# A fifth batch of early keys and values, and a shorter last routing, in a two-layer decoder kernel on one core

## The chip, the core and the metric

The kernel runs on one core of a Trainium2 chip. A core has five engines that each work through their own queue in order: TensorE (PE in the profile; its weight loads are shown as PEld) multiplies matrices and transposes, VectorE (DVE), ScalarE (ACT) and GpSimd (POOL) work on elements, and SyncE (SP) mostly issues DMAs. They wait for each other by semaphores. The metric is the device time of one execution in microseconds (us), taken as the median of several runs. Everything here is computed in 32-bit floating point; the profile shows each such matmul as two records, so "x8" in a matmul row is four matmuls.

## The reference

The input `x` has 16 batches of 112 tokens with 256 features, the context `ctx` 16 batches of 375 rows. Two pre-norm layers follow each other; the change lies in the second layer, and around the place where the two meet. Cut to what matters:

```python
x = x + L0_attn(layernorm(x))               # linear attention
x = x + L0_xattn(layernorm(x), ctx)         # 16 heads
x = x + L0_ffn(layernorm(x))                # 16 experts, top 2, plus a shared one
x = x + L1_attn(layernorm(x))               # 16 heads of 64
x = x + L1_xattn(layernorm(x), ctx, g1, b1, g2, b2, Wq, Wkv, Wout, bout)   # 8 heads of 64
x = x + L1_ffn(layernorm(x))                # 8 experts, top 2, capacity 33

def L1_xattn(x, context, ...):
    xn, cn = layer_norm(x, g1, b1), layer_norm(context, g2, b2)
    q = xn @ Wq
    k, v = split(cn @ Wkv, 2)               # per batch: 375 x 512 each
    return softmax(q k^T / 8) v @ Wout + bout

def L1_ffn(x, ...):                         # per batch of 112 tokens
    top, ei = top_k(x @ router_w + router_b, 2)
    probs = softmax(top)
    pos = place of the token in its expert's list (first choices of all tokens come first)
    buf[ei, pos] = x                        # 8 experts x 33 places; later ones are dropped
    out[e] = silu((buf[e] @ w_c_fc + b) * (buf[e] @ w_gate + b)) @ w_c_proj + b
    return sum over the two choices of probs * out[ei, pos]
```

## The kernel before

The residual `x` stays in on-chip memory, with 112 tokens on the partitions. The stages run one after another over the 16 batches.

**Layer 0's experts and the join.** Tokens are gathered into blocks of 128 rows of one expert each; 36 blocks (`NB_MEAN`) are worked through by `blocks(0)` in a hand-written order for PE and DVE (`fetch`, `turn`, `up`, `turn_act`, `down`): SP loads a block (`xb`), PE multiplies, ACT scales the result (`os`), and POOL scatters its rows to DRAM (`yo`, by `scatter`, line 1063). Behind it stands `If n_used > NB_MEAN`, which on these inputs isn't taken; each engine loads the count and branches. Then the pools of this stage are closed, and layer 1 opens its own in the same memory. Layer 1 begins with `combine(b)` (line 1530): SP loads the two rows of each token back (`yb`), DVE adds them to `x`, and the norm of layer 1 follows (`norm_one`: line 234 and 235 on DVE, 242 and 243 on POOL, 238 on DVE, the transposes of line 267 on PE).

**Keys and values ahead.** The keys and values of layer 1's cross-attention depend on `ctx` alone. For the batches in `AHEAD` (0, 4, 8, 12) they are computed during layer 0, with `c_ahead` (three transposes and one ACT operation per half), `k_ahead` (four pieces of two matmuls, copied by ACT, line 401) and `v_ahead` (three pieces of two matmuls, line 414), and ACT stores them to DRAM (`kd`, `vd`; lines 403 and 416). `norm_ahead` norms the context rows.

**Layer 1's cross-attention.** It has 32 units, two per batch (`n` counts them, `u` is 0 or 1), each for four heads. In the loop at line 1600 and on, a unit emits: `turned` (transposes of the probabilities, line 1493), `scores` of the next unit (line 1461; then the row maximum on DVE, line 1472, exp on ACT, line 1473, the reciprocal on DVE, line 1482, and the division of the 112x375 probabilities on POOL, line 1484, four per unit), one entry popped from the list `after`, the projection of the batch before (`project`), the query pieces, the pieces that make the next batch's keys and values if it isn't in `AHEAD` (`c_piece`, `k_piece`, `v_piece`: six transposes of the context, 8 key and 6 value matmuls per batch over two units), and `values` (line 1509). If the next batch is in `AHEAD`, SP loads its keys and values instead (`k_load`, `v_load`).

**Routing.** The list `after` holds the routing work: `routed(b)` (router logits of batch b; after every fourth batch also `route1`, the top two of eight), `places` (the place of each token in its expert, from two prefix-sum matmuls and, per rank k, a chain of small DVE operations), and `dispatch1(b)` for four batches, which builds a 112x264 matrix of ones (`dm`, from `slot_rows`) and multiplies it by the normed tokens (`xn`), so that the tokens land at their places (`first_in` for the first 12 places of every expert, `more_at` for the other 21). `places` also sums, per expert, how many tokens stand beyond the first 12 (`more`, `need`); `ranks` orders the experts by that count, and SP needs its result to load the weights of the four busiest experts. The last routing comes after the units: what is left in `after`, `routed(15)`, `places`, `slot_rows`, `ranks` and `dispatch1` of batches 12 to 15, and then the first expert (`hidden`, from line 1826 on). `jobs` is a list of small tasks, one popped per step of the expert loop. The order on PE and DVE in these parts is that of the code.

## Time and profile before

| | us |
|---|---|
| median of three runs (1603.69 to 1607.48) | 1604.29 |
| time of the profiled execution | 1611.35 |
| its span | 1609.6 |
| PE busy | 1501.8 (93%) |
| DVE busy | 964.1 (60%) |
| ACT busy | 577.9 |
| POOL busy | 483.1 (30%) |
| last matmul of layer 0's blocks ends | 608.4 |
| first matmul of layer 1 | 621.0 |
| last projection of the cross-attention ends | 1316.7 |
| first matmul of the first expert | 1342.7 |

The span is the time from the first to the last instruction of one profiled execution, and the times in the rows below are counted from its start. The clock granted to PE was 0.973 of full speed on average. In a timeline row stand: start, duration, engine, line of the code, operation, what it writes and reads, its shape, how many instructions are taken together, and in brackets how long the engine had been idle and what ended that. A row of a queue (SPq, ACTq) is the issue of a DMA, not its transfer.

### The profile page before, as it was taken

The numbers are of one execution on the slowest core, as the hardware profiler recorded it, in microseconds if no ns is written. First come the engines' busy times: TensorE is split into PE (matmuls) and PEld (weight loads), VectorE is DVE, ScalarE is ACT, GpSimd is POOL, SyncE is SP. The second block draws the span as 40 slices with busy tenths as digits, with TensorE's granted clock in tenths as the row PEclk, the third lists the DMA queues.
The fourth block names the chain that finished last, engine by engine and source line by source line (L and its number), as shares of the span: only waits on it lengthen the run. The fifth ranks groups of instructions, "written<-read, shape, count | busy, mean of one in ns | idle before, by whom it ended". The sixth has DMA issues, their size and how long they took to land.

```text
span 1609.6 us, 30346 instructions
## 1 busy us (share of the span) xinstructions
PE 1501.8 (93%) x11438; PEld 1127.5 (70%) x11438; DVE 964.1 (60%) x2649; ACT 577.9 (36%) x1437; POOL 483.1 (30%) x647
## 2 busy tenths in 40 slices
PE   7898999999988896899999989999999978999998
PEld 5776777777754585778888756666666657788786
DVE  6986777777762353976677655566575566342124
ACT  3441444444442252223333233343434323333332
POOL 5642122222115352323333344544445420000000
PEclk9999999999999897999999999999999988999999
DMA  6500322222224476200000010101010012344421
GB/s 170 143 10 21 94 67 65 67 65 65 64 76 158 130 231 214 54 24 1 1 1 2 20 56 10 49 20 48 19 30 30 1 53 79 137 178 157 147 89 48
DMA packets 84929, 116.52 MB, mean 72 GB/s; under 512 B 13433, under 2 KB 70946, under 8 KB 84778
## 3 DMA queue, kind: packets, MB, share of 16 engines
q1 hardware_dynamic: 78690, 98.25, 20.1%
q0 software_dynamic: 3312, 8.54, 1.6%
q10 hardware_dynamic: 2776, 7.72, 1.4%
q8 instruction: 95, 1.56, 0.4%
q14 instruction: 56, 0.46, 0.1%
HBM read 84.41 MB, written 22.08 MB: 66 GB/s over the span
## 4 chain that ended last, share of the span: by engine, by line
PE 76%; DVE 13%; POOL 4%; DMA 3%; issue 2%; another core or an unknown queue 1%; ACT 1%; SPq 0%; POOLq 0%; DVEq 0%; ACTq 0%
PE pT L120 49%; PE pT L785 3%; PE pT L1461 3%; PE pT L1493 2%; POOL pr L1484 2%; DVE mx L769 2%; PE pT L1509 2%; PE pT L803 2%; PE pT L767 2%; PE pT L1358 2%; PE pT L1393 2%; PE pT L1379 2%; PE pT L620 1%; DVE st L234 1%
## 5 line engine op out<-in xcount | busy, mean ns | idle before, releaser
L1484 POOL TENSOR_SCALAR pr<-pr,den 112x375 f32<-112x375 f32 x128 | 157.0, 1244 | 176.9 <-DVE den L1482 157.7
L120 PE MATMUL pT<-xnT,w_all 128*128 128x224 f32 (+2 forms) x800 | 165.3, 358 | 0.6 <-DVE xnT L269 0.5
L120 PEld LDWEIGHTS pT<-xnT,w_all 128*128 128x128 f32 x800 | 145.9, 197 | 10.2 <-issue 5.7
L794 ACT ACTIVATE pr<-pT 125x336 f32<-125x336 f32 x256 | 94.6, 456 | 126.3 <-PE pT L785 126.3
L769 DVE TENSOR_REDUCE mx<-pT 112x1 f32<-112x375 f32 x256 | 122.2, 539 | 11.3 <-PE pT L767 9.9
L1371 POOL TENSOR_TENSOR pr<-pr,den 112x448 f32<-112x448 f32 x64 | 59.9, 956 | 198.8 <-DVE den L1369 147.9
L120 PE MATMUL pT<-w_all 128*128 (+3 forms) x376 | 113.1, 453 | 1.7 <-ACT w_all L392 0.8
L120 PE MATMUL pT<-w_all,cT 128*125 128x256 f32 (+1 forms) x336 | 111.4, 475 | 0.0
L120 PE MATMUL pT<-cT,w_all 128*128 128x375 f32 x320 | 110.2, 486 | 0.0
L120 PE MATMUL pT<-w_all,xnT 128*112 128x256 f32 (+1 forms) x320 | 105.7, 477 | 1.9 <-ACT xnT L566 0.9
L120 PE MATMUL pT<-w_all,oT 128*112 128x256 f32 x448 | 106.4, 383 | 0.6 <-DVE oT L1400 0.6
L242 POOL TENSOR_SCALAR nr<-nmv 112x1 f32<-112x1 f32 x96 | 22.3, 232 | 273.7 <-DVE nmv L235 273.1
L1308 ACT COPY pT<-pT 112x448 f32<-112x448 f32 (+1 forms) x64 | 34.0, 532 | 170.9 <-PE pT L1493 88.3
L120 PEld LDWEIGHTS pT<-w_all 128*128 128x128 f32 (+2 forms) x376 | 70.2, 190 | 33.8 <-issue 4.6
L1473 ACT ACTIVATE pr<-pT,top 112x375 f32<-112x375 f32 x128 | 72.4, 572 | 56.8 <-DVE top L1472 54.4
L120 PEld LDWEIGHTS pT<-cT,w_all 128*128 128x128 f32 x320 | 59.3, 190 | 41.1 <-issue 5.8
L120 PEld LDWEIGHTS pT<-w_all,oT 128*112 128x112 f32 x448 | 75.7, 177 | 16.3 <-DVE oT L1400 1.0
L120 PE MATMUL pT<-first_in,w_all 128*128 128x192 f32 x512 | 86.6, 329 | 0.0
L120 PEld LDWEIGHTS pT<-first_in,w_all 128*128 128x128 f32 x512 | 84.4, 192 | 1.5 <-issue 0.3
L120 PEld LDWEIGHTS pT<-w_all,cT 128*125 128x125 f32 x336 | 61.1, 187 | 33.3 <-issue 22.7
L120 PEld LDWEIGHTS pT<-w_all,xnT 128*112 128x112 f32 x320 | 57.1, 183 | 35.8 <-issue 22.4
L1767 DVE SCALAR_TENSOR_TENSOR hT<-pT,vT,gt 128x192 f32<-128x192 f32 x64 | 26.7, 417 | 90.5 <-ACT gt L1766 90.4
(306 smaller groups left out, 3019.2 us busy)
## 6 DMA issues: line engine op xcount, KB each, us to landing
w_all<-in_L_ffn_w_c_fc_dram SPq DMA_DIRECT2D x12, 1024.0 KB
w_all<-in_L_ffn_w_gate_dram SPq DMA_DIRECT2D x12, 1024.0 KB
w_all<-in_L_ffn_w_c_proj_dram SPq DMA_DIRECT2D x12, 1024.0 KB
cx<-in_ctx_dram SPq DMA_DIRECT2D x32, 375.0 KB
kz<-kn SPq DMA_DIRECT2D x128, 46.9 KB
xg<-w_all SPq DMA_DIRECT2D x1, 5547.0 KB
xb<-xg SPq DMA_DIRECT2D x36, 129.0 KB
yb<-yo SPq DMA_DIRECT2D x16, 224.0 KB
```

The source lines that it names most:

```text
L120: mm(o, l, r, start=(i == 0), stop=(i == len(terms) - 1))
L767: mm(ps[i][:L, :S], qz[b % 2][r, g, :], kz[b % 2][r, g, :], start=True, stop=True)
L769: nc.vector.tensor_reduce(mx[b % 2][:, g, i, 16:17], ps[i][:L, :S], AX.X, ALU.max, negate=True)
L785: mm(pw[i][:KC, j * L : (j + 1) * L], kz[b % 2][r, g, j * KC : (j + 1) * KC], qm[r, :], start=True, stop=True,)
L794: nc.scalar.activation(pr[:, i, :], pw[i][:KC, : NKC * L], AF.Exp)
L803: mm(po[32 * i : 32 * i + 32, :L], va[b % 2][:, j, 4 * g + i, :], pr[:, i, j * L : (j + 1) * L], start=(j == 0), stop=(j == NKC - 1),)
L1308: nc.scalar.copy(dst, src)
L1358: mm(ps[k][:L, s * L : (s + 1) * L], q, kk, start=True, stop=True)
L1371: nc.gpsimd.tensor_tensor(pr[:, k], pr[:, k], bcast(den[:, k, :], L), ALU.mult)
L1461: mm(ps[2 * s + k][:L, :S], qTs[b // 2][rows(k), m, (b % 2) * L : (b % 2 + 1) * L], kTs[b][rows(k), m, :], start=True, stop=True,)
L1473: nc.scalar.activation(pr[:, i, :], ps[i][:L, :S], AF.Exp, bias=top[:, i : i + 1], scale=1.0, accum_out=den[:, i : i + 1],)
L1484: nc.gpsimd.tensor_scalar(pr[:, n, :], pr[:, n, :], den[:, n : n + 1], None, ALU.mult)
```

## The change

It has two parts. First, batch 2 joins `AHEAD`, as its fifth entry (index 4). Its keys and values are made around the join: `Wkv` is loaded a second time into a part of `xnT` that is free then, the context rows are normed during the blocks, `c_ahead` stands in the last rounds of `blocks(0)`, two key pieces before the `If`, two key pieces and the three value pieces after it. In the cross-attention, batch 1's units load batch 2's keys and values instead of making them.

Second, `places` is split. What the dispatches need stays (with `place` counted from 1, so that a subtraction goes; `kept`, the place cut at 32, moves to POOL), and the probabilities and the counts (`more`, `sums`, `need`) go to a new entry `counts`, which comes after the dispatches in the list. From unit 28 on, two entries are popped per unit. In the last routing POOL norms the tokens of batches 12 to 14, and `counts` and `ranks` become tasks of the first expert. For batch 15 the tokens normed before are used.

```diff
@@ -68,7 +68,7 @@
         "rev16": rows(E0 - np.arange(E0)),
         "rev8": rows(E1 - np.arange(E1)),
         "io8": rows(np.arange(E1)),
-        "slots": rows(np.arange(E1 * CAP)),
+        "slots": rows(np.arange(E1 * CAP + 1)),
 
         "later": np.concatenate(
             [
@@ -356,7 +356,7 @@
 
 
 
-    AHEAD = (0, 4, 8, 12)
+    AHEAD = (0, 4, 8, 12, 2)
     kd = {b: dr.tile([128, 4, S], F32, tag=f"kd{b}", name=f"kd{b}") for b in AHEAD}
     vd = {b: dr.tile([KC, NKC, 512], F32, tag=f"vd{b}", name=f"vd{b}") for b in AHEAD}
 
@@ -381,7 +381,7 @@
         if c == 0:
             acTs[i] = (
                 kap[0].tile([128, 2, S], F32, tag="acT", name="acT", bufs=1)
-                if i % 2
+                if i % 2 or i == 4
                 else w_all[:, 2 * WR + 4864 : 2 * WR + 4864 + 2 * S].rearrange("p (c s) -> p c s", c=2)
             )
         pt = bank()
@@ -397,7 +397,7 @@
         if m == 0:
             akv[i] = kz[0] if i == 0 else kap[0].tile([128, 4, S], F32, tag="ak", name="ak")
         pk = bank()
-        mm_sum(pk[:, :S], [(wkv_a[0][:, c, m * 128 : (m + 1) * 128], acTs[i][:, c, :]) for c in range(2)])
+        mm_sum(pk[:, :S], [(wkv_a[i // 4][:, c, m * 128 : (m + 1) * 128], acTs[i][:, c, :]) for c in range(2)])
         nc.scalar.copy(akv[i][:, m, :], pk[:, :S])
         if m == 3:
             nc.scalar.dma_start(kd[AHEAD[i]], akv[i])
@@ -410,18 +410,18 @@
                 else kap[0].tile([KC, NKC, 512], F32, tag="av", name="av")
             )
         pv = bank()
-        mm_sum(pv[:KC, :], [(acTs[i][:, c, j * KC : (j + 1) * KC], wkv_a[0][:, c, 512:]) for c in range(2)])
+        mm_sum(pv[:KC, :], [(acTs[i][:, c, j * KC : (j + 1) * KC], wkv_a[i // 4][:, c, 512:]) for c in range(2)])
         nc.scalar.copy(akv[i][:, j, :], pv[:KC, :])
         if j == NKC - 1:
             nc.scalar.dma_start(vd[AHEAD[i]], akv[i])
 
     ahead = [
         f
-        for i in range(len(AHEAD))
+        for i in range(4)
         for f in (
             [lambda i=i, m=m: k_ahead(i, m) for m in range(4)]
             + [lambda i=i: v_ahead(i, 0)]
-            + [lambda i=i, c=c: c_ahead(i + 1, c) for c in range(2)] * (i + 1 < len(AHEAD))
+            + [lambda i=i, c=c: c_ahead(i + 1, c) for c in range(2)] * (i < 3)
             + [lambda i=i, j=j: v_ahead(i, j) for j in (1, 2)]
         )
     ]
@@ -1103,6 +1103,11 @@
                     if j in (12, 17, 22):
                         with tc.issue_after(got.ins):
                             w_qkv.extend(load_w(2 * WR + 2048 * i, [t["L1_attn_W_qkv"][i]]))
+                    if j == 24:
+
+                        wkv_a.append(xnT[:, :, NT - 1024 :])
+                        with tc.issue_after(got.ins):
+                            nc.sync.dma_start(wkv_a[1], rows_of(t["L1_xattn_Wkv"]))
 
             def turn(j):
                 pt = bank()
@@ -1153,16 +1158,27 @@
                         turn_act(n - 2)
                     if begin <= n - 3:
                         down(n - 3)
+                    if begin == 0 and n == stop - 6:
+                        norm_ahead(4)
+                    if begin == 0 and n in (stop, stop + 1):
+                        c_ahead(4, n - stop)
 
 
             w_qkv = []
             stop = NB_MEAN
             blocks(0)
+            for m in range(2):
+                k_ahead(4, m)
         n_used = nc.values_load(used[0:1, 0:1], min_val=0, max_val=NB0)
         with tc.If(n_used > NB_MEAN):
             with tc.manual_schedule(engines={mybir.EngineType.PE, mybir.EngineType.DVE}):
                 stop = NB0
                 blocks(NB_MEAN)
+        with tc.manual_schedule(engines={mybir.EngineType.PE}):
+            for m in range(2, 4):
+                k_ahead(4, m)
+            for j in range(NKC):
+                v_ahead(4, j)
     cstack.close()
     f0s.close()
     rp = pool(ctx, "route", 1)
@@ -1223,13 +1239,6 @@
         bs = slice(4 * q, 4 * q + 4)
         (oh0, v0), (oh1, v1) = top_two(lp, lg1[:, bs, :], E1, const("rev8", L))
 
-        p0, ex = prob[0][:, bs], prob[1][:, bs]
-        nc.vector.tensor_sub(ex, v1, v0)
-        nc.scalar.activation(ex, ex, AF.Exp)
-        nc.vector.tensor_scalar(p0, ex, 1.0, None, ALU.add)
-        nc.vector.reciprocal(p0, p0)
-        nc.vector.tensor_mul(ex, ex, p0)
-
         oh = [o.rearrange("p b n -> p (b n)") for o in (oh0, oh1)]
 
         def places():
@@ -1239,9 +1248,8 @@
             mm_sum(pc[:L, 4 * E1 : 8 * E1], [(before, oh[1]), (ones[:L, :L], oh[0])])
             b1 = lambda name: lp.tile([L, 4], F32, tag=f"rt_{name}", name=name, bufs=1)
             tmp = lp.tile([L, 4, E1], F32, tag="rt_tmp", name="tmp", bufs=1)
-            sums = lp.tile([L, E1], F32, tag="rt_sums", name="sums", bufs=1)
             for k in range(2):
-                pos, ok, more = b1(f"pos{k}"), b1(f"ok{k}"), b1(f"more{k}")
+                pos, ok = b1(f"pos{k}"), b1(f"ok{k}")
                 o3 = (oh0, oh1)[k]
                 kept, ei = pos1[k][:, bs], exp1[k][:, bs]
                 nc.vector.tensor_tensor(
@@ -1252,18 +1260,32 @@
                 nc.vector.tensor_reduce(ei, tmp, AX.X, ALU.add)
                 nc.vector.tensor_scalar(ok, pos, CAP - 0.5, None, ALU.is_lt)
 
-                nc.vector.tensor_scalar(kept, pos, float(CAP - 1), None, ALU.min)
-
-                nc.vector.scalar_tensor_tensor(pos, ei, float(CAP), kept, ALU.mult, ALU.add)
-                nc.vector.scalar_tensor_tensor(pos, pos, 1.0, ok, ALU.add, ALU.mult)
-                nc.vector.tensor_scalar(place[k][:, bs], pos, -1.0, None, ALU.add)
-
-                nc.vector.tensor_scalar(more, kept, P0 - 0.5, None, ALU.is_gt)
-                nc.vector.tensor_tensor(tmp, o3, bcast(more, E1), ALU.mult)
+                to = place[k][:, bs]
+                nc.vector.scalar_tensor_tensor(to, ei, float(CAP), pos, ALU.mult, ALU.add)
+                nc.vector.scalar_tensor_tensor(to, to, 1.0, ok, ALU.add, ALU.mult)
+
+                nc.gpsimd.tensor_scalar(kept, pos, float(CAP - 1), None, ALU.min)
+
+        def counts():
+
+            p0, ex = prob[0][:, bs], prob[1][:, bs]
+            nc.vector.tensor_sub(ex, v1, v0)
+            nc.scalar.activation(ex, ex, AF.Exp)
+            nc.vector.tensor_scalar(p0, ex, 1.0, None, ALU.add)
+            nc.vector.reciprocal(p0, p0)
+            nc.vector.tensor_mul(ex, ex, p0)
+
+            b1 = lambda name: lp.tile([L, 4], F32, tag=f"rt_{name}", name=name, bufs=1)
+            tmp = lp.tile([L, 4, E1], F32, tag="rt_tmp", name="tmp", bufs=1)
+            sums = lp.tile([L, E1], F32, tag="rt_sums", name="sums", bufs=1)
+            for k in range(2):
+                more = b1(f"more{k}")
+                nc.vector.tensor_scalar(more, pos1[k][:, bs], P0 - 0.5, None, ALU.is_gt)
+                nc.vector.tensor_tensor(tmp, (oh0, oh1)[k], bcast(more, E1), ALU.mult)
                 nc.vector.tensor_reduce(sums, tmp.rearrange("p b n -> p n b"), AX.X, ALU.add)
                 nc.vector.tensor_add(need, need, sums)
 
-        return places
+        return places, counts
 
     def dispatch1(lp, b, made=None):
 
@@ -1278,14 +1300,15 @@
             copy(first_in[:, c, :, :, b], src[:, :, :P0])
             copy(more_at[:, c, :, :, b], src[:, :, P0:])
 
-    def slot_rows(lp, b):
-        slots = const("slots", L)
+    def slot_rows(lp, b, xn=None):
+        slots = const("slots", L)[:, 1:]
         dm = lp.tile([L, E1 * CAP], F32, tag="dm", name="dm", bufs=2)
         d1 = lp.tile([L, E1 * CAP], F32, tag="d1", name="d1", bufs=1)
         nc.vector.tensor_scalar(d1, slots, place[0][:, b : b + 1], None, ALU.is_equal)
         nc.vector.scalar_tensor_tensor(dm, slots, place[1][:, b : b + 1], d1, ALU.is_equal, ALU.add)
-        xn = lp.tile([L, D], F32, tag="xn", name="xn", bufs=2)
-        normed(xn, x[:, b, :], mv1[:, b, 0:1], r1[:, b : b + 1])
+        if xn is None:
+            xn = lp.tile([L, D], F32, tag="xn", name="xn", bufs=2)
+            normed(xn, x[:, b, :], mv1[:, b, 0:1], r1[:, b : b + 1])
         return dm, xn
 
 
@@ -1591,10 +1614,11 @@
                 logits1(b)
                 if b % 4 == 3:
                     q = b // 4
-                    places = route1(rp, q)
+                    places, counts = route1(rp, q)
                     after.append(places)
                     if q < B // 4 - 1:
                         after.extend(lambda b=b: dispatch1(lp, b) for b in range(4 * q, 4 * q + 4))
+                    after.append(counts)
 
             units = [(b, u) for b in range(B) for u in range(2)]
             for n, (b, u) in enumerate(units):
@@ -1609,8 +1633,9 @@
                 if b + 1 in AHEAD and u == 0:
                     k_load(b + 1)
                     v_load(b + 1)
-                if after:
-                    after.pop(0)()
+                for _ in range(2 if n > 27 else 1):
+                    if after:
+                        after.pop(0)()
                 if late and n:
                     flush(0)
                     if b:
@@ -1826,16 +1851,25 @@
 
         with tc.manual_schedule(engines={mybir.EngineType.DVE, mybir.EngineType.PE}):
             late.pop(0)()
-            while after:
+            xns = {}
+            for b in range(B - 4, B - 1):
+                xns[b] = lp.tile([L, D], F32, tag="xn", name="xn", bufs=3)
+                nc.gpsimd.tensor_scalar(
+                    xns[b], x[:, b, :], mv1[:, b, 0:1], r1[:, b : b + 1], ALU.subtract, ALU.mult
+                )
+            xns[B - 1] = xn15
+            after.pop(0)()
+            while len(after) > 1:
                 after.pop(0)()
-            made = {b: slot_rows(lp, b) for b in (B - 4, B - 3)}
-            ranked = ranks()
+            made = {b: slot_rows(lp, b, xns[b]) for b in (B - 4, B - 3)}
             for b in range(B - 4, B):
                 dispatch1(lp, b, made.pop(b))
                 if b + 2 < B:
-                    made[b + 2] = slot_rows(lp, b + 2)
-            jobs = bias_of(0)
-            jobs += share_jobs(share_first, KA, first_idx)
+                    made[b + 2] = slot_rows(lp, b + 2, xns[b + 2])
+            ranked = []
+            jobs = [after.pop(0)] + share_jobs(share_first, KA, first_idx)
+            jobs.insert(4, lambda: ranked.extend(ranks()))
+            jobs[5:5] = bias_of(0)
             for r in range(1, RANKS):
                 jobs += bias_of(r)
             jobs += share_jobs(share_more, KL, lambda k: more_idx(k, 0))
```

## The prediction

> **What bounds the kernel now.** I read the page's chain of waits first, then the timelines of the three places the diff touches: the layers' join, the late units of the second layer's cross-attention, and the way from the last router logits to the first expert.
>
> ```profile
> PE 76%; DVE 13%; POOL 4%; DMA 3%; issue 2%; another core or an unknown queue 1%; ACT 1%; SPq 0%; POOLq 0%; DVEq 0%; ACTq 0%
> ```
>
> TensorE (PE) carries the chain, but not at these places. The join, by the timelines of ACT, POOL, SP and PE:
>
> ```profile
> 608.41 0.47 ACT L1135 ACTIVATE os<-pT,xb 128x256 f32<-128x256 f32 x1 [0.17 <-issue]
> 610.40 0.96 POOL L1063 DMA_INDIRECT yo<-os,to  x1 [0.30 <-issue]
> 613.90 0.81 SPq L1530 DMA_DIRECT2D yb<-yo  x2
> 620.98 0.61 PE L267 MATMUL pT<-call,xn 112*128 112x112 f32 x2 [12.61 <-DVE nmv L235]
> ```
>
> PE stops at 608.4, POOL issues the last row scatter at 610.40, SP the first `yb` load at 613.90, PE goes on at 620.98. What PE does within these 12.6 us is free only if that load isn't made later.
>
> In the cross-attention, the view of windows shows three units that begin with a batch whose keys and values were made ahead, and then three that all make some (columns: window, its length, busy time with instruction count of PE, its weight loads, DVE, ACT, POOL, then granted clock):
>
> ```profile
> 1027.00:1058.20 31.20, 28.22 (x194) 20.00 (x194) 16.06 (x42) 12.07 (x36) 16.12 (x16) 0.95 0.10 37
> 1058.20:1094.30 36.10, 36.10 (x221) 23.93 (x220) 25.76 (x89) 13.90 (x41) 15.41 (x14) 1.00 0.04 12
> ```
>
> The making stretch is full of PE work; the other is not, yet is only 4.9 us shorter.
>
> **Join: part 1 of the change, what it adds.** Batch 2's keys and values go here. Making one batch's costs PE 11.7 us by the timeline: six transposes 0.86, 16 records of 375 columns 5.38 (two rows of 2.69 for 8), 12 of 512 columns 5.49 (1.88 for 4, 3.61 for 8). Of it, the transposes and key pieces 0 and 1 stand before the `If`, pieces 2 and 3 and the three value pieces after it, and ACT stores keys and values to DRAM. In the built program's order SP's first `yb` load then waits for both stores to land, which it did not before: the pool that the pieces were copied through is closed there, and its memory is `yb`'s. So the question is when the value store lands. A like store earlier in the same execution:
>
> ```profile
> 545.28 0.58 ACT L414 COPY av<-pT 125x512 f32<-125x512 f32 x1 [2.67 <-PE pT L120]
> 545.90 0.26 ACTq L416 DMA_DIRECT2D vd<-av  x1
> 554.07 0.99 POOL L1063 DMA_INDIRECT yo<-os,to  x1 [14.43 <-DMA vd<-av]
> ```
>
> By the DMA view of that stretch its queue moves 60 to 250 GB/s from 546.6 to 553.0, so the data is down 7.1 us after the issue (keys: 2.6, issued 471.4, done 474.0).
> Timeline: PE 608.4 + 0.86 + 2.69 = 611.9; ACT's copy 0.47, 612.4. The way through the `If`: unknown, between 0 and the 3.5 us that POOL spends from the end of its last scatter to its next row (614.84); SP's own run of passed waits before 613.90 is 0.7, the nearest, so 1.0: 613.4. Then 2.69 + 3 x 1.88 = 8.3 of PE, 621.7; last copy 0.59; store 7.1: 629.4 against 613.90, **+15.5**.
> The clock adds to that. A stretch of 3.4 us with little PE work is followed by half clock:
>
> ```profile
> 1303.90:1307.40 3.50, 2.14 (x14) 1.61 (x12) 3.02 (x19) 0.53 (x1) 3.42 (x5) 1.00 0.00 0
> 1307.40:1310.80 3.40, 0.49 (x1) 0.50 (x2) 3.07 (x10) 0.00 (x0) 0.26 (x1) 0.51 0.00 0
> ```
>
> PE busy 2.14 of 3.5 us, and the next stretch is granted 0.51. The `If` leaves one with about 1.9 busy; the next 3.4 us then do half: +1.7. The half clock after the join (0.50 until 628.2 now) stays as it is, only later. **Join +17.2**; bounds +13.8 (no time in the `If`, store 6.4, clock kept) and +25 (`If` 3.5, store landed only at 554.07, all 8.3 us at half clock).
> The Trainium skill, "DMA: Bandwidth & Descriptors", section "Anatomy of one DMA — SWDGE (gpsimd) path", puts a fixed cost of about 2 us on a DMA, most of it the receipt of the last write, longest towards HBM; the trace shows last bytes, not receipts. By that rule, an estimate, the join would be +19. "Advanced Engine Details and Errata", section "Control Flow Timing", has 108 ns for a compare-and-branch, so about +16.3 with my 1.0 replaced; no row shows either.
> The second load of `Wkv` (1 MB) lies in a stretch where three loads of 1 MB stand already among the block fetches while the scatters keep 1.63 us spacing: 0. Three DVE normings at block 30: 0.41 each, at most 1.2, under PE's pace.
>
> **Cross-attention: what part 1 removes.** PE has 11.7 us less in batch 1's two units. But without it they're bound by the loop max, exp, POOL's four divisions (4.86 per unit), transposes: POOL starts at 1030.14, 1039.80, 1049.48, 9.7 us apart, and the backlog is paid in the next unit. The windows give 36.1 - 31.2 = 4.9, and the next pair (1117.7 and 1149.3) 36.3 - 31.6 = 4.7: **-5**, bounds -4 and the whole -11.7.
>
> **Routings inside the cross-attention.** `kept` goes to POOL, and in the built order DVE's `more` waits for it right after `ok`; `kept` stands behind two, then four, of POOL's divisions, and the next reciprocal and `place` stand behind `more`. In routing 0 and 1 (units 11 and 22) this delays the divisions by about 2 us once: unit 11 is PE-bound, unit 22 isn't: +0.5, bounds 0 and 3. The dispatches of batches 4 to 7 move from units 21 to 24 (two of them POOL-bound) to 23 to 26 (one POOL-bound): one more of 1.2 us on PE-bound units: **+1.2**, bounds 0 and 2.4.
>
> **Unit 30, where the pops double.** Now:
>
> ```profile
> 1300.10 0.78 PE L120 MATMUL pT<-oh,call 112*112 112x32 f32 x6
> 1300.71 1.96 PE L120 MATMUL pT<-w_all,oT 128*112 128x256 f32 x8
> 1302.60 1.37 PE L1509 MATMUL pT<-pT,vt 125*64 125x112 f32 x24
> ...
> 1310.31 2.10 PE L1275 MATMUL pT<-dm,xn 112*128 112x264 f32 x4 [2.94 <-DVE xn L238]
> ...
> 1301.79 4.94 POOL L1484 TENSOR_SCALAR pr<-pr,den 112x375 f32<-112x375 f32 x4 [6.07 <-DVE den L1482]
> ```
>
> After: dispatch(8) stands in PE's queue ahead of project(14) (1.96) and values (1.37), and waits for `dm(8)`. Two divisions end at 1304.2; `kept` 0.23 (price of POOL's L242), `more` 1304.6, so the second reciprocal moves from 1302.80 to 1304.9, the divisions end at 1307.4, second `kept` 1307.7, then two `place`, one `dm`: 1309.2. PE idles from 1300.75, 8.5 us, and is at half clock until 1314.3 (first full stretch 1310.8). In PE's order: dispatch 2.1 (1311.3), project(14) 3.4 (1314.7), values 1.4, transposes 1.5 (1317.6), dispatch(9) 1.06, (10) 0.9 wait + 1.06 (1320.7), L267 0.4, values 1.4, copy 0.4 + project(15) 2.0: 1324.8 against 1316.73: **+8.1**, bounds +5 (clock kept) and +11.
>
> **After project(15).**
>
> ```profile
> 1323.16 0.61 PE L267 MATMUL pT<-call,w_all 112*128 112x112 f32 x2
> 1327.90 0.95 PE L120 MATMUL pT<-oh,call 112*112 112x32 f32 x4 [0.70 <-DVE oh L301]
> 1334.75 3.70 PE L1275 MATMUL pT<-dm,xn 112*128 112x264 f32 x8 [0.55 <-PE pT L1660]
> 1342.73 2.49 PE L120 MATMUL pT<-first_in,w_all 128*128 128x192 f32 x7
> ```
>
> Two dispatches fewer stand ahead of L267, but POOL's three normings (0.73 by its 112x256 addition L1604, 1.24 by its 112x375 division; 0.83 by columns) stand ahead of batch 15's L242: L267 comes 5.1 us after project(15) instead of 6.4: -1.3 (0 to -2). Places: now first `tmp` 1328.89 to dispatch 1334.71, 5.8; per rank four DVE operations on the path and two small ones drop out, and no norming: 3.45: -2.4. Dispatches: 8.0 us with the ranking between; without, four at half clock, 4 x 1.88 = 7.5: -0.5 (-2 at full clock). The ranking's 2.2 us and the counts' 2.7 go into unit 0's 13 us on DVE, which is busy 3 to 6 tenths there in the page's slices; if that cover is gone, unit 1's weight load starts late, up to 1. **Tail -4.2**, bounds -1.5 and -6.5.
>
> **Sum.** +17.2 - 5 + 0.5 + 1.2 + 8.1 - 4.2 = +17.8 on the profiled span of 1609.6 (its time 1611.35): 1627.4. The median of the runs is 1604.29; the difference carries over: **1622**. I tell faster or slower from no change by 0.3%, 4.8 us.
>
> **Rivals.**
> The first `yb` load is not held (not slower): if the stores land before the scatters' own landing lets SP go, the join costs 0 and the sum is +0.6, 1605. For it: PE idles 12.6 us there. Against: 8.3 us of PE and a 7.1 us store begin only after the `If`. It decides from a join below +4.2. Chance 0.05.
> The whole of PE's 11.7 us comes out of the cross-attention: +11.1, 1615. Against: the two windows. 0.08.
> Unit 30 hides its stall, PE taking project(14) in time: -8.1, so +9.7, 1614. Against: the built order. 0.12.
> The join at half clock through all its pieces, a store that lands at the late bound: +25, 1630. 0.13.
> The change doesn't do what it says at the tail, since dispatches at half clock and POOL's normings take it back: 0 instead of -4.2, 1626. 0.1.
> The forecast as summed, 1617 to 1627: 0.52.
> Same 0.07 and faster 0.03 come from the first rival and from several terms at their low bounds together; all else is slower, 0.9. Range 1610 to 1631: the second and third rivals nearly whole, the fourth in half.
>
> **What would show it.** After's first `yb` load near 629 to 632, right behind the landing of the value store, PE's L267 some 7 us later; batch 1's three units near 31.3 us; in unit 30 a PE gap of 8 us ahead of the dispatch's matmuls ended by DVE's `dm`; first `first_in` matmuls about 22 us after project(15) ends instead of 26. Wrong if `yb` issues before 620, or if PE's gap in unit 30 is under 4 us.

## The result and the profile after

The changed kernel took 1625.87 us, the median of 4 runs (1621.88 to 1635.62), against 1603.99 for the kernel before on the same chip: a ratio of 1.0142, 95% interval 1.0094 to 1.0189. It is slower by about 22 us, with 15 to 30 in the interval. A later comparison of the same two kernels gave 1.0093 (1.0077 to 1.0109), some 15 us.

The profiled execution after has a span of 1624.0 us, at a mean granted clock of 0.969. That is only 14.4 us more than the span of the profiled execution before, because that one lost several us in layer 0 ahead of every edit (under "What stays open"): its last block matmul ends at 608.4, that of the kernel after at 604.9. So I cut both traces at the same instructions and compare what lies between. Each row below runs from one landmark to the next, read from the PE timeline.

| stretch (us) | before | after | after - before | predicted |
|---|---|---|---|---|
| join: last block matmul to layer 1's first | 12.61 | 26.52 | +13.9 | +17.2 |
| layer 1's self-attention, to the first cross scores | 328.04 | 326.28 | -1.8 | 0 |
| first scores to `values` of unit 1 | 28.39 | 28.42 | 0 | 0 |
| `values` of unit 1 to 4 (batch 1 begins them) | 36.24 | 32.30 | -3.9 | -5 |
| `values` 4 to 20 | 180.82 | 180.79 | 0 | 0 |
| `values` 20 to 29 | 101.39 | 106.14 | +4.8 | +1.7 |
| `values` 29 to the end of project(15) | 20.87 | 29.84 | +9.0 | +8.1 |
| end of project(15) to the first expert | 26.00 | 22.22 | -3.8 | -4.2 |
| experts to the last matmul | 261.00 | 260.13 | -0.9 | 0 |

The rows add up to +17.3. In the block stage ahead of them 3.9 us more were lost, behind the second `Wkv` load (below); the two make 21.2, against the 21.9 between the medians.

The join, by the timelines of PE, ACT's queue, SP's queue and POOL of the kernel after:

```profile
608.62 2.79 PE L120 MATMUL pT<-acT,xnT 128*128 128x375 f32 x8 [1.18 <-ACTq L1173]
611.25 5.31 PE L120 MATMUL pT<-xnT,acT 128*125 128x512 f32 x12
617.22 0.50 ACTq L416 DMA_DIRECT2D vd<-av  x1
624.91 5.23 SPq L1553 DMA_DIRECT2D yb<-yo  x4
625.55 0.61 POOL L1324 DMA_DIRECT2D bout<-in_L_xattn_bout_dram  x1 [18.02 <-DMA vd<-av]
631.44 0.61 PE L267 MATMUL pT<-call,xn 112*128 112x112 f32 x2 [14.88 <-DVE nmv L235]
```

PE has finished the added pieces at 616.6 and then stands idle for 14.88 us. The bracket behind L267 names DVE, but that is only the last link. ACT issues the value store at 617.22, and SP's first `yb` load, which used to be free to start after the scatters, is issued 7.7 us later. POOL's row, waiting 18.02 us, names the cause outright: `DMA vd<-av`. The view of SP's own waits names it too: 9.3 us for `vd<-av` there, a wait that the kernel before doesn't have.

Unit 30, by PE's and POOL's timelines of the kernel after:

```profile
1309.62 0.78 PE L120 MATMUL pT<-oh,call 112*112 112x32 f32 x6
1318.59 2.10 PE L1297 MATMUL pT<-dm,xn 112*128 112x264 f32 x4 [8.19 <-DVE dm L1308]
1320.48 3.07 PE L120 MATMUL pT<-w_all,oT 128*112 128x256 f32 x8
```

```profile
1311.31 2.46 POOL L1507 TENSOR_SCALAR pr<-pr,den 112x375 f32<-112x375 f32 x2 [6.45 <-DVE den L1505]
1313.85 0.22 POOL L1267 TENSOR_SCALAR pos<-pos 112x4 f32<-112x4 f32 x1
1314.54 2.48 POOL L1507 TENSOR_SCALAR pr<-pr,den 112x375 f32<-112x375 f32 x2 [0.46 <-DVE den L1505]
1316.99 0.22 POOL L1267 TENSOR_SCALAR pos<-pos 112x4 f32<-112x4 f32 x1
```

The dispatch of batch 8 now heads PE's queue, and PE waits 8.19 us for its matrix `dm`. Project(14), which was ready, runs only behind it, and mostly at half clock (3.07 us instead of 1.96; the granted clock is 0.50 from 1318.50 to 1320.50 and 0.61 in the 3 us after). POOL shows why `dm` is late: each 0.22 us minimum (`kept`, L1267) stands behind two divisions of 1.2 us.

### The profile page after: what moved, and what is told of

It reads as the page before. It is cut to its first block, busy times and chain, and to the rows that moved or that the text cites. A ratio compares the mean times of both kernels' runs of the same rounds, so it can differ in the third digit from the quotient of the medians.

```text
span 1624.0 us, 30348 instructions
## 1 busy us (share of the span) xinstructions
PE 1506.9 (93%) x11438; PEld 1129.3 (70%) x11438; DVE 957.9 (59%) x2626; ACT 580.6 (36%) x1440; POOL 489.5 (30%) x658
## 3 DMA queue, kind: packets, MB, share of 16 engines
q8 instruction: 95, 1.56, 0.4%
## 4 chain that ended last, share of the span: by engine, by line
PE 52%; POOL 4%; DVE 3%; DMA 1%; ACT 1%; issue 1%; POOLq 0%; ACTq 0%; DVEq 0%; SPq 0%
PE pT L120 36%; POOL pr L1507 3%; PE pT L1484 3%; PE pT L1516 2%; PE pT L1532 2%; PE pT L1381 2%; PE pT L1416 2%; PE pT L1402 2%; PE pT L1297 1%; PE pT L1832 1%; DMA cx<-in_ctx_dram 1%; ACT pr L1496 1%; PE pT L1453 1%; PE pT L267 1%; POOL pr L1394 0%
## 5 line engine op out<-in xcount | busy, mean ns | idle before, releaser
L120 PE MATMUL pT<-w_all,cT 128*125 128x256 f32 (+1 forms) x324 | 105.9, 471 | 0.0
L120 PE MATMUL pT<-cT,w_all 128*128 128x375 f32 x304 | 104.4, 485 | 0.0
L120 PEld LDWEIGHTS pT<-w_all,xnT 128*112 128x112 f32 x320 | 56.3, 180 | 34.9 <-issue 22.9
L120 PE MATMUL pT<-hT,w_all 128*128 128x192 f32 (+1 forms) x384 | 79.7, 366 | 0.0
## 6 DMA issues: line engine op xcount, KB each, us to landing
kz<-kn SPq DMA_DIRECT2D x128, 46.9 KB
```

Of the source, the lines that this page charges most:

```text
L120: mm(o, l, r, start=(i == 0), stop=(i == len(terms) - 1))
```

## The experiments

All ratios are to the kernel before on the same chip, with 95% intervals; under each edit stands what was expected before the run. The first four kernels split the loss by place.

**join_only.** The kernel before with the fifth batch alone.

```diff
-    AHEAD = (0, 4, 8, 12)
+    AHEAD = (0, 4, 8, 12, 2)
...
+            for m in range(2):
+                k_ahead(4, m)
...
+            for m in range(2, 4):
+                k_ahead(4, m)
+            for j in range(NKC):
+                v_ahead(4, j)
```

> Part 1 alone: batch 2 in AHEAD, the routing as before. My theory (the first yb load waits for the value store): first matmul of layer 1 about 26 us after the last block's matmul instead of 12.6, +14; batch 1's units give back 4; so +10 on before, about 1614. Rival (the pieces fill the idle time of the join and cost nothing): -4, about 1600.

1624.56 us, 1.0050 (1.0033 to 1.0068). The join took 26.40 us, so all of the join's loss belongs to the fifth batch; batch 1's units took 32.21 instead of 36.24. The units from 20 to 29, project(15) and the tail lie at 103.54, 21.53 and 25.70, near the values of before.

**route_only.** The kernel after without the fifth batch.

```diff
-    AHEAD = (0, 4, 8, 12, 2)
+    AHEAD = (0, 4, 8, 12)
```

> Part 2 alone: the routing and the last routing changed, four batches ahead as before. My theory: units 20 to 29 +5 (the waits for kept, dispatches in units that TensorE bounds), unit 30 and 31 +9, from project(15) to the first expert -4; so +10 on before, about 1614. Rival (the whole loss comes from the join): about 1602 to 1605.

1621.29 us, 1.0037 (1.0022 to 1.0052). Join 12.36; `values` 20 to 29 104.52, `values` 29 to project(15) 29.81, tail 22.40. The shortened last routing works, but the loss in unit 30 takes back more than twice its gain. The two halves sum to 1.0087, inside the interval of the whole in its second comparison and just under that of the first (from 1.0094). No interaction of the two is to be seen.

**free_join.** Is it the PE work at the join, or the wait for the store? The fifth batch's pieces get memory of their own (a free part of `xnT` and of the weight buffer), and all of its key and value pieces stand behind the `If`. PE has the same work; `yb` has nothing to wait for.

```diff
-                kap[0].tile([128, 2, S], F32, tag="acT", name="acT", bufs=1)
-                if i % 2 or i == 4
+                xnT[:, :, 384 : 384 + S]
+                if i == 4
...
-            akv[i] = kz[0] if i == 0 else kap[0].tile([128, 4, S], F32, tag="ak", name="ak")
+            akv[i] = (
+                kz[0]
+                if i == 0
+                else w_all[:, 2 * WR - 3072 : 2 * WR - 3072 + 4 * S].rearrange("p (m s) -> p m s", m=4)
...
```

> The changed kernel with batch 2's pieces all after the If and copied through memory that layer 1's first loads do not take (acT in xnT, ak and av in the weights' second third). The work stays, the wait of the first yb load for the two stores goes. My theory: TensorE's 10.9 us of pieces fit into the 12.6 us that it idles anyway, the join costs 0 to 1 and the clock stays full, so 14 to 17 less than the changed kernel, 1609 to 1612. Rival (the pieces' own time on TensorE is the cost): first matmul of layer 1 not before 20 us after the last block, at most 6 less.

1627.08 us, 1.0069 (1.0041 to 1.0097). PE and SP of free_join:

```profile
610.05 10.46 PE L120 MATMUL pT<-xnT 128*128 128x375 f32 x28 [1.18 <-ACTq L1181]
621.88 0.38 PE L267 MATMUL pT<-call,xn 112*128 112x112 f32 x2 [1.37 <-issue]
628.15 9.21 PE L120 MATMUL pT<-xnT,w_all 128*128 128x224 f32 x32 [4.34 <-DVE xnT L269]
```

```profile
614.19 6.38 SPq L1561 DMA_DIRECT2D yb<-yo  x4
```

The join is back at 13.02 us though PE now works through 10.46 us of it. So the price of the join is the wait, and there the work alone is nearly free. But of the 14 to 17 us that were expected little came: from the last block matmul to the last matmul this execution is only 2.7 us shorter than after's. The largest part went behind the join: the next row of PE waits 4.34 us for `xnT`, and the self-attention took 333.85 us, where all the other kernels took 326.0 to 329.6. On DVE the first copy of `xnT` (L269) now stands at 627.33, behind the additions and norms of batches 2 and 3. That is tested below (best_all).

**late_disp8.** Unit 30 without the doubled pop.

```diff
-                for _ in range(2 if n > 27 else 1):
+                for _ in range(2 if n in (28, 29, 31) else 1):
```

> The changed kernel with one entry popped in unit 30 instead of two, so that dispatch(8) stands in unit 31 and dispatch(10) behind the units. My theory (TensorE's queue is held by dispatch(8) in front of project(14) and values): no gap of 8 us in unit 30, project(15) 7 us earlier, 1 to 2 given back by the dispatch behind the units: 5 to 7 less than the changed kernel, about 1620. Rival (the divisions held by the wait for kept are what delays unit 30): the gap moves to the transposes, at most 2 less.

1626.79 us, 1.0058 (1.0036 to 1.0081). PE of late_disp8:

```profile
1323.44 0.78 PE L120 MATMUL pT<-oh,call 112*112 112x32 f32 x6
1324.05 1.96 PE L120 MATMUL pT<-w_all,oT 128*112 128x256 f32 x8
1325.94 1.37 PE L1532 MATMUL pT<-pT,vt 125*64 125x112 f32 x24
...
1335.18 2.10 PE L1297 MATMUL pT<-dm,xn 112*128 112x264 f32 x4 [3.70 <-DVE xn L238]
```

Project(14) follows the prefix sums at once and the 8 us gap is gone, but not the loss: it moves to the next unit, where the transposes wait for POOL's divisions (1.46 and 0.63 us) and the dispatch for `xn` (3.70). From `values` 29 to the first expert it is 45.0 us, against 52.1 after and 46.9 before. So the order alone makes of a loss of 5.2 us there a gain of 1.8: 7.0 us less than after, where 5 to 7 were expected. It isn't the whole of what the routing can give, since `kept` still stands behind POOL's divisions in this kernel.

**kept_dve.** `kept` back on DVE in the kernel after, nothing else.

```diff
-                nc.gpsimd.tensor_scalar(kept, pos, float(CAP - 1), None, ALU.min)
+                nc.vector.tensor_scalar(kept, pos, float(CAP - 1), None, ALU.min)
```

> The changed kernel with kept computed on DVE instead of POOL, nothing else. My theory (DVE's more waits behind POOL's divisions for kept, in every routing inside the units): unit 22 to 23 back from 10.4 to 7.4 or 8.5 us, the second reciprocal of unit 30 two us earlier, so the gap in front of dispatch(8) about 5.5 instead of 8.2 us and project(15) 2 to 3 us earlier: in all 5 to 6 less in these stages. Rival (the gap in unit 30 is dispatch(8)'s place in the queue alone): unit 22 the same as in the changed kernel, or unit 30 within 1 us of it.

1618.86 us, 1.0072 (1.0050 to 1.0094). The gap of PE ahead of the dispatch in unit 30:

```profile
1310.96 2.10 PE L1297 MATMUL pT<-dm,xn 112*128 112x264 f32 x4 [5.25 <-DVE dm L1308]
```

5.25 instead of 8.19 us: 2.9 us of the stall are `kept` behind POOL's divisions, the rest is the dispatch ahead of project(14). From `values` 22 to 23 it took 8.48 us against 10.40 (7.43 before), so `kept` costs 1.9 us there too.

**best_route.** The two repairs together, without the fifth batch: route_only with `kept` on DVE and the pops of late_disp8.

```diff
-                for _ in range(2 if n > 27 else 1):
+                for _ in range(2 if n in (28, 29, 31) else 1):
...
-                nc.gpsimd.tensor_scalar(kept, pos, float(CAP - 1), None, ALU.min)
+                nc.vector.tensor_scalar(kept, pos, float(CAP - 1), None, ALU.min)
```

> Part 2 alone, with kept on DVE and one entry popped in unit 30. My theory: units 20 to 29 as before (101 to 103 us), values of unit 29 to the first expert 44 to 45 us against 46.9 before and 52.1 with the whole change: 2 to 3 us faster than before, ratio 0.998 to 0.999. Rival (the shortened chain itself is worth nothing): that stretch 47 us or more.

1605.65 us, 0.9985 (0.9972 to 0.9997): faster than the kernel before by 2.4 us, as expected, but by less than the 0.3% that I count as a difference. From `values` 29 to project(15) 23.54, tail 19.68: 43.2 us together against 46.9. PE of best_route at the tail:

```profile
1320.44 0.57 PE L267 MATMUL pT<-call,w_all 112*128 112x112 f32 x2 [2.40 <-DVE w_all L238]
1329.77 5.06 PE L1281 MATMUL pT<-dm,xn 112*128 112x264 f32 x12 [3.68 <-DVE dm L1292]
1335.69 6.89 PE L120 MATMUL pT<-first_in,w_all 128*128 128x192 f32 x40
```

From L267 to the first expert 15.25 us, where it was 19.57 before. Against the 3.7 us won behind `values` 29, the units 20 to 29 take 2.8 more than before (104.22 against 101.39); 1.8 of them lie in one stretch that varies between executions (`values` 23 to 24, below).

**best_all.** best_route and free_join together, and the order of DVE at the join written out.

```diff
-        with tc.manual_schedule(engines={mybir.EngineType.PE}):
-            for b in range(4):
+        with tc.manual_schedule(engines={mybir.EngineType.PE, mybir.EngineType.DVE}):
+            for b in range(2):
...
+            flush(0)
+            for b in range(2, 4):
+                got = combine(b)
+                late.append(norm_one(lp, b))
+        with tc.manual_schedule(engines={mybir.EngineType.PE}):
```

> The same routing with batch 2's pieces after the If, copied through memory that layer 1's first loads do not take, and DVE's order around the join written out so that the first xnT copy comes before the additions of batches 2 and 3. My theory: join 12.6 to 14 us, layer 1's attention 326 to 329 us instead of the 334 of the earlier attempt, units 1 to 4 at 32 us, the end as in the kernel with the mended routing: 5 to 7 us faster than before, ratio 0.996. Rival (the pieces cannot be hidden at the join, the time comes back in the attention): attention 332 us or more, ratio 1.000 or above.

1605.63 us, 0.9991 (0.9974 to 1.0009): no difference from before. DVE of best_all, the first copy:

```profile
619.84 0.41 DVE L238 TENSOR_SCALAR xn<-x_res,nmv,nr 112x256 f32<-112x256 f32 x1 [0.99 <-POOL nr L243]
620.16 0.38 DVE L269 COPY xnT<-pT 128x224 f32<-128x224 f32 x1
```

The copy comes right behind the second batch's norm, the join takes 12.60 us and the self-attention 326.74. So the order on DVE was the rest of free_join's loss around the join. From the last block matmul to the last matmul this execution is 8.6 us shorter than before's; 3.9 of them were lost again ahead of it, in the blocks behind the second `Wkv` load. And it is the fastest of twelve (1599.77), so its stages flatter the kernel. The 5 to 7 us that were expected did not come. Beside best_route at 0.9985, the fifth batch gains nothing that can be told even with the join mended: the 3.9 us that batch 1's units give back are about what the fourth load costs.

**before_again.** The kernel before, unchanged, with a profile.

> The kernel before once more, for a second profile. If the stall of 11.8 us in layer 0's experts in its first profile (ACT waiting with a remote cause, TensorE idle from 516.5 to 528.2) belongs to the kernel, it is there again; if it comes and goes by execution, the time of the last block's matmul differs by several us between executions of one kernel, and totals should be compared from that point on.

1607.33 us, 0.9993 (0.9983 to 1.0004). It shows how steady the stages are: join 12.76, batch 1's units 36.25, `values` 29 to project(15) 20.93, tail 25.85, all within 0.2 us of the first profile. But `values` 4 to 20 took 184.08 against 180.82, the same code with other stretches at half clock. The stall in layer 0 that is told under "What stays open" differs too.

**xn_early.** POOL's three norms stand ahead of batch 15's own in its queue. Here two of them are issued before project(15), into memory of their own, and the third goes to DVE.

```diff
+        xns = {B - 4: None}
+        for b in range(B - 3, B - 1):
+            xns[b] = w_all[:L, 3 * WR - (B - b) * D : 3 * WR - (B - 1 - b) * D]
+            nc.gpsimd.tensor_scalar(
...
-            for b in range(B - 4, B - 1):
-                xns[b] = lp.tile([L, D], F32, tag="xn", name="xn", bufs=3)
```

> The changed kernel with POOL's normings of batches 13 and 14 made ahead of project(15), into free columns of the weights' memory, and that of batch 12 left to DVE, so that batch 15's rstd (L242, L243) finds POOL free. My theory (three normings of 1.22 us each stand in front of it): the router's transpose L267 comes 3 to 4 us after project(15) instead of 6.2, project(15) to the first expert 19.5 to 20.5 instead of 22.2. Rival (the router's logits of batches 13 and 14 or the dispatch hold TensorE there): less than 1 us.

One run, 1629.18 us, too little for a ratio. The stage from project(15) to the first expert took 18.76 us, 3.5 less than after (3.2 less than after_again). L267 waits 1.42 us instead of 4.59:

```profile
1345.22 0.38 PE L267 MATMUL pT<-call,w_all 112*128 112x112 f32 x2 [1.42 <-DVE w_all L238]
```

**wkv_27.** Are the two late blocks behind the second `Wkv` load a matter of where it is put? Three blocks later:

```diff
-                    if j == 24:
+                    if j == 27:
```

> The changed kernel with the second load of Wkv issued behind block fetch 27 instead of 24, so that it does not follow the load behind fetch 22 at two blocks. My theory (two 1 MB loads close together hold the block fetches back): the longest spacing of the scatters after the fifteenth falls from 2.2 to 5.6 us to at most 2.5, blocks 61.6 or 65 us long as in the kernel before plus 0.5. Rival (any fourth load costs it): a spacing of 3 us or more some blocks later.

One run, 1633.57 us, too little for a ratio. Its scatters at the load are 5.41 and 2.87 us apart, against 4.62 and 2.49 after: the theory that the place matters falls. The stall is only put off by three blocks.

**after_again.** The kernel after, unchanged, beside these.

> The changed kernel once more, beside the others on one chip. By the stages of its first trace it should be 17 to 19 us slower than before, ratio 1.010 to 1.012; the first measurement's middle of 1.014 would hold too much of layer 0's coming and going.

1632.36 us, 1.0093 (1.0077 to 1.0109). That is just under the 1.010 to 1.012 expected. Join 26.52 and `values` 29 to project(15) 28.77 are near the first profile; the self-attention (329.38), `values` 1 to 4 (34.43) and `values` 4 to 20 (183.33) are each 2 to 3 us longer in the same kernel. So a change of that size in these three stages is not told by one profile.

**best_final.** best_all with xn_early's norms and wkv_27's place.

```diff
-                    if j == 24:
+                    if j == 27:
...
+        xns = {B - 4: None}
+        for b in range(B - 3, B - 1):
...
```

> The kernel with the mended routing and the mended join, with these two mends as well. My theory: join 12.6, attention 327, units 1 to 4 32.3, units 20 to 29 103 to 104, values of unit 29 to the first expert 40 to 42 against 46.9 before, blocks at most 1 us longer than before: 8 to 10 us faster than before, ratio 0.994 to 0.995. Rival (what is gained at the end is lost again in the experts or to TensorE's clock): ratio 0.998 or above.

1613.31 us, 0.9980 (0.9963 to 0.9997). Best_route and this one are the only two whose interval lies below 1, by 0.15 to 0.2%, which is under what I count as a difference. Of the 8 to 10 us expected about 3 came, and the sign given for the rival (0.998 or above) was met. The end came as forecast: `values` 29 to the first expert took 41.9 us, with a tail of 18.67, and the join took 12.68. But the blocks took 65.3 us from the first to the last scatter, against 56.3 and 57.6 in the two profiles of before, where 1 us more was expected; the loss at the `Wkv` load is the largest of all, with scatters 6.29 and 2.99 us apart. The self-attention (329.6) and `values` 1 to 4 (34.5) were over their forecast too, in an execution that is the slowest of the twelve.

## Why the prediction came out

**The total.** 1622 was forecast, on the slower side, and 1625.87 came, inside the range. By stages it is +21.2 against the +17.8 of the sum. The place and the cause of each large term of the sum were right. Several sizes were not: the join came 3.3 us below its term, while the inner routings came 3.1 and the `Wkv` load 3.9 us above theirs. That these partly cancel, and that the total came so near, is luck.

**The join, +17.2 predicted, +13.9 measured.** The mechanism is as told: SP's first load waits for the value store, and free_join shows that without this wait the same PE work costs 0.4 us at the join. Counted from the last block matmul, the first `yb` issue was put 21.0 us later and came at 20.0. The value store lands 7.7 us after its issue, close to the 7.1 that was taken from the earlier store. Passing the `If` costs PE 1.18 us, close to the 1.0. The pieces were done sooner than reckoned (11.7 us after the last block matmul instead of 13.3), since the six transposes lie among the last blocks and ACT's copy is not in the chain. So of the 3.3 us that the join came below its forecast, 1.0 is the earlier issue, 0.6 a shorter way from there to L267 (6.5 instead of 7.1), and 1.7 the clock's term, which fell whole. Windows of the kernel after at this place:

```profile
606.80:610.20 3.40, 2.22 (x8) 1.09 (x7) 0.00 (x0) 0.48 (x2) 0.73 (x1) 1.00 0.22 84
610.20:613.60 3.40, 3.40 (x10) 1.69 (x9) 0.00 (x0) 1.37 (x3) 0.00 (x0) 1.00 0.26 106
```

PE is busy 2.22 of 3.40 us in the stretch with the `If`, and the next keeps a clock of 1.00. I had reckoned with 1.9, and the row with 2.14 that was followed by half clock lies closely below. The upper bound of +25 was added wrongly: its own terms make 15.5 + 2.5 + 1.1 + 8.3 = 27.4. The Trainium skill's "DMA: Bandwidth & Descriptors", section "Anatomy of one DMA — SWDGE (gpsimd) path", with its fixed 2 us would have given +19 by the estimate in the prediction. That section speaks of DMAs issued by GpSimd; this store is issued by ACT. The trace shows bytes from about 617.8 to 624.2 and SP's issue at 624.91, so less than 1 us lies between the last byte and the release.

**Cross-attention, -5 predicted, -3.9 measured.** Batch 1's units give back 3.9 us and not the 11.7 us of PE work. Without that work PE waits there for POOL's divisions, as the two windows of before had suggested (in the kernel after, three waits of 0.63 us and one of 0.83 in one unit's transposes), and the rival by which all 11.7 come out is refuted. Across the kernels with the fifth batch the gain is 1.7 to 5.0 us.

**Routings inside, +1.7 predicted, +4.8 measured.** Here the +0.5 for `kept` was mis-sized. From `values` 22 to 23 alone 2.97 us were lost (10.40 against 7.43), at the upper bound of 3; kept_dve gives back 1.92 of them. The other 1.05 goes with the moved `places`, as far as the traces tell: it stands in unit 22 now, where it stood in unit 20 before, and the trace of kept_dve has PE waiting in several small places behind it (the transposes take 1.95 us instead of 1.56, the rest are waits of 0.1 to 0.2 us around the query pieces). POOL's timelines show the 1.92, before first, then after, then kept_dve:

```profile
1222.27 5.00 POOL L1484 TENSOR_SCALAR pr<-pr,den 112x375 f32<-112x375 f32 x4 [4.27 <-DVE den L1482]
1230.97 4.87 POOL L1484 TENSOR_SCALAR pr<-pr,den 112x375 f32<-112x375 f32 x4 [3.71 <-DVE den L1482]
```

```profile
1221.79 0.22 POOL L1267 TENSOR_SCALAR pos<-pos 112x4 f32<-112x4 f32 x1
1222.89 0.22 POOL L242 TENSOR_SCALAR r<-mv 112x1 f32<-112x1 f32 x1 [0.87 <-DVE place L1265]
1229.02 4.95 POOL L1507 TENSOR_SCALAR pr<-pr,den 112x375 f32<-112x375 f32 x4 [5.22 <-PE pT L120]
1238.72 4.87 POOL L1507 TENSOR_SCALAR pr<-pr,den 112x375 f32<-112x375 f32 x4 [4.75 <-DVE den L1505]
```

```profile
1225.94 4.98 POOL L1507 TENSOR_SCALAR pr<-pr,den 112x375 f32<-112x375 f32 x4 [5.21 <-PE pT L120]
1234.63 4.87 POOL L1507 TENSOR_SCALAR pr<-pr,den 112x375 f32<-112x375 f32 x4 [3.71 <-DVE den L1505]
```

The idle time ahead of the second unit's divisions is 4.75 us with `kept` on POOL and 3.71 with it on DVE, which is also what the kernel before has there. The divisions are 9.70 and 8.69 us apart (8.70 before), so 1.0 of the 1.92 us is read directly from this. The stretch from `values` 23 to 24 was 1.86 us longer after than before (16.44 against 14.58), but it is 14.81 in route_only, which has the same routing there, and 16.22 in join_only, which has the old one: it varies between executions, and the routing is not its cause. That leaves +3.0 for the routing. The other seven stretches, where the dispatches moved, change by -0.9 to +0.5 and by -0.1 in sum, so the moved dispatches, put at +1.2, cost nothing there.

**Unit 30, +8.1 predicted, +9.0 measured.** The gap of 8.19 us ended by `dm` is the predicted 8.5, and project(14) ran mostly at half clock. The rival that hides the stall needs PE to take project(14) first; late_disp8 did just that and gained 4.4 us at project(15) over after (25.45 against 29.84), and 7.0 up to the first expert.

**The tail, -4.2 predicted, -3.8 measured.** L267 came 6.2 us after project(15), not 5.1: POOL's three norms were priced at 0.83 us each and took 1.22.

```profile
1336.28 3.65 POOL L1857 TENSOR_SCALAR xn<-x_res,mv,r 112x256 f32<-112x256 f32 x3 [10.63 <-DVE st L234]
1339.91 0.23 POOL L242 TENSOR_SCALAR r<-mv 112x1 f32<-112x1 f32 x1
1341.40 0.61 PE L267 MATMUL pT<-call,w_all 112*128 112x112 f32 x2 [4.59 <-DVE w_all L238]
1350.53 5.62 PE L1297 MATMUL pT<-dm,xn 112*128 112x264 f32 x12 [3.45 <-issue]
```

The step that was to give -1.3 gave -0.2. The places gave -2.5 (predicted -2.4) and the dispatches -1.1 (predicted -0.5). xn_early shows that POOL's queue was the price: with its norms out of the way the tail is 18.76. The ranking and the counts, hidden in the experts by the prediction, cost nothing there (-0.9).

**The second `Wkv` load, 0 predicted, +3.9 measured.** This was argued from three like loads among the blocks that cost nothing, and it is wrong: with the fourth, blocks come late, and wkv_27 shows that the place of the loss moves with the load. (Nor are the three quite free: in the four traces without the fourth, one spacing of the scatters there is 1.87 to 3.11 us.) SP's queue and POOL's scatters of the kernel after:

```profile
572.43 0.45 SPq L1110 DMA_DIRECT2D xnT<-in_L_xattn_Wkv_dram  x1
573.68 20.45 SPq L1100 DMA_DIRECT2D xb<-xg  x11
```

```profile
580.75 0.96 POOL L1063 DMA_INDIRECT yo<-os,to  x1 [0.67 <-ACT os L1140]
585.37 0.96 POOL L1063 DMA_INDIRECT yo<-os,to  x1 [3.65 <-ACT os L1140]
587.86 0.96 POOL L1063 DMA_INDIRECT yo<-os,to  x1 [1.53 <-DVE bxT L1117]
589.49 0.96 POOL L1063 DMA_INDIRECT yo<-os,to  x1 [0.67 <-DVE bxT L1117]
```

The scatters stand 1.63 us apart and twice 4.62 and 2.49, so 3.9 us are lost; PE waits at 580.98 with "DMA xb<-xg" as the releaser. The other kernels with the load lost between 0.8 (kept_dve) and 6.0 us (best_final, with the load three blocks later) there. Why this load costs so much more than the three before it, and so differently, stays open; no run here changed the block fetches around it.

**What stays open.** In nine of the fourteen traced executions, one of before's two and one of after's two among them, PE waits 7.6 to 11.8 us in layer 0's shared experts (before's first profile, 528.22: 11.77 us for DVE `sg`). In the other five this wait is missing, and the blocks then wait 4.2 to 4.3 us for their first loads instead. At the last block matmul 6 to 7 us of it are left (608.4 and 608.1 with it, 601.2 and 601.8 without, in the kernels without the fourth load). It lies ahead of every moved instruction, so it belongs to no edit. The eight traces of two later chips all have it and the four of a third don't, and before's median is 7.6 to 8.0 us higher on those two (1615.62 and 1616.05 against 1608.06); but in the first comparison before's profile has it and after's hasn't. Its cause stays open. It is why I compare stages; whether it is also why +21.9 and +15 came out for the same kernel, no run here shows.

## What to carry to other kernels

Work put into an idle stretch is free only if the memory it uses, and the transfers it starts, hold up nothing behind it: look for the first load of the next stage and for what releases its buffer. A small operation given to an engine with long instructions in its queue can cost their length, not its own, when another engine waits for its result. An order of issue that puts a waiting instruction ahead of ready work cost here both the wait and half the clock for some us afterwards. And a load that is put among others because those seemed free has to be tried by itself: this one took back about all that the fifth batch gave.

## What the runs showed of the hardware

A store of 750 KB of values from 125 partitions took 7.7 us from its issue to the release of its waiter, at 98 to 141 GB/s and about a third of the DMA engines busy. The key store, of the same size from 128 partitions, was down 2.6 us after its issue in the kernel before; in the kernel after, where it is issued at 611.95, its bytes flow from about 612.6 to 614.8, at up to 420 GB/s. No run changes the number of partitions alone.

POOL takes 1.22 us for a subtract-and-multiply with two per-partition scalars on 112x256 elements, where its 112x256 addition takes 0.73 and the same norm on DVE 0.41.

The stretch with PE busy 2.22 of 3.40 us was followed by a granted clock of 1.00, the one with 2.14 of 3.50 by 0.51. The rows here don't say where between them, or by what else, that is decided.
